# Local attention in a fused decoder: exponentials taken from PSUM, the mask as a factor, output projections at the ends of blocks

## The chip, the core and the metric

The kernel runs on one core of one Trainium2 chip, as one launch. The metric is device time in microseconds, here the median of three runs. A core has engines that run side by side, each working through its own queue in order: TensorE (PE, matrix products; its weight loads are listed apart as PEld), VectorE (DVE), ScalarE (ACT), GpSimd (POOL) and SyncE (SP, which issues DMAs here). PE writes its results to PSUM[...]; DVE and ACT read them from there and write to SBUF.

## What is computed

A decoder with two layers over x of 8 x 512 x 256: layer 0 is self attention, cross attention and a "feed-forward" part that is itself a small transformer of depth 2 with local attention; layer 1 is a quantized attention, a media cross attention and a mixture of experts. All in float32. The change touches the local attention alone, which runs twice:

```
h = shift_token(x); q, k, v = split(h @ wqkv)            # 8 heads of 64
q, k = rotary_xpos(l2norm(q) * qs, l2norm(k) * ksc)
# windows of 128 rows; each query sees its own window and the one before
sim  = einsum(q * 8, k)
mask = (i < j) | (i > j + 128) | (j == -1)
attn = softmax(where(mask, -max, sim))
x = x + (attn @ v) @ wo
```

Since q and k are normalized, the scores are bounded, and the kernel takes no maximum before the exponential.

## The kernel before

The kernel is written with a framework that orders each engine's instructions at build time: it takes those that are ready by its own estimate, by priority, which falls in the order in which the program issues them. Three helpers steer it. `high_priority(AT_ONCE)` lifts instructions over all others. `together` keeps a group of matmuls in one piece behind its first. `in_turn` puts the PE instructions of a thunk behind the newest PE instruction issued so far. Work of a later group that is ready can still be placed ahead of earlier work that is not.

`local_attention(l, y, ahead)` (L1844) is called for l = 0 and 1. It walks 32 blocks, four per batch row (8 rows of the batch; n = 64 heads, two per block). In block `pair` the loop at the end does three things:

- `scores` for two heads of this block (L2017 on): 8 matmuls (16 records, since a float32 matmul is made as two) into two PSUM tiles "sc" of two banks each, keys by queries in tiles of 128 with their 256 (or 128) queries. For each of the two tiles DVE adds the mask (0 or 1e30, L2036, at once) and writes "la_e" to SBUF; ACT makes exp(-x) of that in place (L2040). The queries carry a factor of -8, so that the minus sign is undone. There are six buffers of la_e.
- `weigh` for the two heads of the block before (L2052 on): 8 matmuls with the values into bank "po" (L2047), a copy of it by ACT (L2064), and after every second block 16 matmuls with ones into bank "sum", whose copy by DVE (L2075) goes by DMA to DRAM. There it is reshaped, inverted (L3326) and read back spread over partitions (L3339); POOL multiplies it onto the values (L3340), which gives "la_oT".
- The next batch row's thunks, some of a list of eight groups, one group for each head of the row's blocks (`prepare`, L1958). They are: `turn`, transposes of the input (L1881) with copies by ACT; `project` (L1890), a projection of 128 rows into 512 columns (L1897), evacuated by ACT twice for queries and keys (a square, L1904, and a copy, L1905) and once for values (L1902); `square` and `root` on DVE for the norms; `rotate` (L1924) on DVE, five long operations (L1932 to L1942); `turn_heads` (L1944), transposes of the rotated rows in two halves of four (L1950), each copied by ACT (L1953). The first blocks of a row hold input transposes and query and key projections; the last two hold four times a value projection followed by two halves of transposes.

All of `turn`, `project`, `turn_heads` and `project_out` take their PSUM from two banks "pj", which change hands in turn.

`later` (class Background, L3386) is a list of delayed thunks: each `tick` counts one and runs at most one that is due. A tick stands before each head's group and after each thunk. The four output projections of a batch row (`project_out`, L2087, one for each 128 rows: 8 matmul records, L2090, and an at-once residual add by DVE, L2096) are put on this list 9, 12, 15 and 18 ticks after the last division has begun. In the steady rows each of them lands just before a value projection and its transposes.

The neighbours are the cross attention before layer 0 (its exponential, L1735, and product, L1736, are of the form that the change brings) and the feed-forward `local_ffn` (L2123) after each layer, whose first pieces are run ahead in the last blocks.

Of the kernel before, what the change touches and what calls it, by code (L numbers as in the profile page):

```python
# [33 lines left out]
AF = mybir.ActivationFunctionType  # L34
ALU = mybir.AluOpType
# [4 lines left out]
P = 128  # L40
B, S, C = 8, 512, 256
NST = S // P
NT = B * NST
EPS = 1e-5
BIG = 1e30
# [1232 lines left out]
class FastDecoder(Decoder):  # L1278
# [565 lines left out]
    def local_attention(self, l, y, ahead):  # L1844
# [3 lines left out]
        nc, t = self.nc, self.t  # L1848
        wqkv, wo = self.load_local_attention(l)
        yield  # L1850
        later = Background()
# [9 lines left out]
        scale = self.alloc(first, [P, 2, 64], F32, "la_scale", bufs=1)  # L1861
# [133 lines left out]
        with self.tc.tile_pool(  # L1995
            reuse_waits="tile", name="la", bufs=2, side=sides[1]
        ) as pool, self.tc.tile_pool(reuse_waits="tile", name="lps", bufs=1, space=PSUM) as psum:
            second = pool
            self.pj = lambda: self.alloc(psum, [P, 512], F32, "pj", bufs=2)
            one, two = [P, 512], [P, 2, 512]  # L2000
            if l:
                self.reserve(psum, ("sc", two, 2), ("pj", one, 2), ("po", one, 1), ("sum", one, 1))
            else:
                self.reserve(psum, ("sum", one, 1), ("po", one, 1), ("sc", two, 2), ("pj", one, 2))


            mask = self.alloc(pool, [P, NST, P], F32, "la_mask", bufs=1)
            nc.gpsimd.memset(mask, 0.0)
            for j in range(NST):
                sign = -1 if j % 2 else 1  # L2010
                nc.gpsimd.affine_select(
                    out=mask[:, j, :], in_=mask[:, j, :], pattern=[[sign, P]], compare_op=ALU.is_ge,
                    fill=BIG, base=0, channel_multiplier=-sign,
                )
            mask = mask.rearrange("p j k -> p (j k)")

            def scores(n):  # L2017

                b, c = divmod(n, 4)
                d = held[b]  # L2020
                both = [self.alloc(psum, [P, 2, 512], F32, "sc", bufs=2) for half in range(2)]
                for m in self.together(8):
                    half, jj, r = m // 4, m // 2 % 2, m % 2
                    j = 2 * half + jj
                    to = min((j + 2) * P, S)
                    rows = slice(64 * r, 64 * r + 64)
                    nc.tensor.matmul(  # L2027
                        both[half][:, r, jj * 256 : jj * 256 + to - j * P],
                        d["qkT"][rows, 4 + c, j * P : (j + 1) * P], d["qkT"][rows, c, j * P : to],
                        start=True, stop=True,  # L2030
                    )
                for half, ps in enumerate(both):
                    n_cols = 384 if half else 512
                    ex = self.alloc(pool, [P, 2, 512], F32, "la_e", bufs=6)
                    with self.tc.high_priority(self.AT_ONCE):
                        nc.vector.tensor_tensor(  # L2036
                            ex[:, :, :n_cols], ps[:, :, :n_cols],
                            mask[:, :n_cols].unsqueeze(1).broadcast_to([P, 2, n_cols]), ALU.add,
                        )
                    nc.scalar.activation(ex[:, :, :n_cols], ex[:, :, :n_cols], AF.Exp, scale=-1.0)  # L2040
                    d["e", 2 * c + half] = ex

            def over_keys(out, lhsT, ex, half, jj):

                j = 2 * half + jj
                to = min((j + 2) * P, S)
                nc.tensor.matmul(  # L2047
                    out[:, j * P : to], lhsT(j), ex[:, jj * 256 : jj * 256 + to - j * P],
                    start=(j == 0), stop=(j == 3), skip_group_check=True,
                )  # L2050

            def weigh(n):  # L2052
                b, c = divmod(n, 4)
                d = held[b]
                d["po"] = self.alloc(psum, [P, 512], F32, "po")
                for m in self.together(8):
                    half, jj, r = m // 4, m // 2 % 2, m % 2
                    at = 128 * c + 64 * r
                    over_keys(
                        d["po"][64 * r : 64 * r + 64, :], lambda j: d["v"][:, j, at : at + 64],  # L2060
                        d["e", 2 * c + half][:, r, :], half, jj,
                    )
                o = d["o", c] = self.alloc(pool, [P, S], F32, "la_o", bufs=3)
                nc.scalar.copy(o, d["po"])  # L2064
                if c % 2 == 0:
                    return
                ps = self.alloc(psum, [P, 512], F32, "sum")
                for m in self.together(16):
                    hf, jj, r = m // 8, m // 4 % 2, m % 4
                    over_keys(  # L2070
                        ps[32 * r : 32 * r + 32, :], lambda j: self.ones[:, :32],
                        d["e", 2 * (c - 1 + r // 2) + hf][:, r % 2, :], hf, jj,
                    )
                total = self.alloc(pool, [P, S], F32, "la_total")
                nc.vector.tensor_copy(total, ps)  # L2075

                def divide(rows):
                    for j in range(2):
                        oT = d["oT", c - 1 + j] = self.alloc(pool, [P, S], F32, "la_oT", bufs=6)
                        self.times_rows(pool, oT, d["o", c - 1 + j], rows[2 * j : 2 * j + 2, :], later)  # L2080
                    if c == 3:
                        for i in range(NST):
                            later.add(9 + 3 * i, lambda i=i: project_out(b, i))

                self.inverted(pool, total[0:P:32, :], later, divide)

            def project_out(b, i):  # L2087
                ps = self.pj()
                for c in range(4):
                    nc.tensor.matmul(  # L2090
                        ps[:, :C], held[b]["oT", c][:, i * P : (i + 1) * P], wo[:, c, :],
                        start=(c == 0), stop=(c == 3),
                    )
                yt = y[:, b * NST + i, :]
                with self.tc.high_priority(self.AT_ONCE):
                    nc.vector.tensor_tensor(yt, yt, ps[:, :C], ALU.add)  # L2096

            n = 8 * B
            ahead.step()
            for pair in range(0, n + 2, 2):  # L2100
                if pair < n:
                    if pair % 8 == 0:
                        ready = prepare(pair // 8 + 1) if pair // 8 + 1 < B else [()] * 8
                    scores(pair // 2)
                if pair >= 2:
                    weigh(pair // 2 - 1)
                for i in (pair, pair + 1):
                    with self.in_turn():
                        later.tick(1)
                    if i < n:  # L2110
                        for thunk in ready[i % 8]:
                            with self.in_turn():
                                thunk()
                                later.tick(1)
                    if i == n - 6:
                        early.close()
                    if i > n - 6:
                        with self.in_turn():
                            ahead.step()
            ahead.step(100)  # L2120
            later.drain()

    def local_ffn(self, l, y, ahead):  # L2123

# [1472 lines left out]
```

## Time and profile before

| what | us |
|---|---|
| median of three runs | 3023.35 (3020.69 to 3023.5) |
| the profiled execution | 3023.1 |
| its span, first to last instruction | 3021.3 |
| PE busy | 2819.4 (93%) |
| DVE busy | 2034.0 (67%) |
| ACT busy | 1192.4 (39%) |
| POOL busy | 386.9 (13%) |
| mask additions L2036, 128 | 135.3 |
| exponentials L2040, 128 | 117.6 |

A row of the profile's groups gives line, engine, operation, what it writes and reads, shapes and count, then busy time and mean ns of one, then the engine's idle time before it and what ended that. A row of waits gives who waited for whom, total us, times and longest. A row of the timeline gives start and length in us, engine and line, and in brackets the idle time before it. PE records are pipelined and their ends modelled, so rows of PE overlap a little.

### The profile page before, as it was taken

The numbers are of one execution on the slowest core, as the hardware profiler recorded it, in microseconds if no ns is written. First come the engines' busy times: TensorE is split into PE (matmuls) and PEld (weight loads), VectorE is DVE, ScalarE is ACT, GpSimd is POOL, SyncE is SP. The second block draws the span as 40 slices with busy tenths as digits, with TensorE's granted clock in tenths as the row PEclk, the third lists the DMA queues.
The fourth block names the chain that finished last, engine by engine and source line by source line (L and its number), as shares of the span: only waits on it lengthen the run. The fifth ranks groups of instructions, "written<-read, shape, count | busy, mean of one in ns | idle before, by whom it ended". The sixth has DMA issues, their size and how long they took to land. (4 is left out here: it accounts for less than half of the span.)

```text
span 3021.3 us, 39786 instructions
## 1 busy us (share of the span) xinstructions
PE 2819.4 (93%) x14944; PEld 1507.2 (50%) x14944; DVE 2034.0 (67%) x4546; ACT 1192.4 (39%) x1687; POOL 386.9 (13%) x357
## 2 busy tenths in 40 slices
PE   8999999979999999999999999999796999997998
PEld 5653333334555556555555556554444344444665
DVE  7458999987767784356776788548797766664110
ACT  2237777745444421134444421114363444441111
POOL 1111111100011010000011011111211012121111
PEclk9999999989999999999999999999898999997999
DMA  7011212101000010001000011001332132313331
GB/s 248 1 35 44 78 50 59 46 25 50 16 22 23 22 28 34 1 1 43 16 23 23 16 46 63 21 17 53 113 126 92 43 106 83 108 58 97 106 138 60
DMA packets 130693, 168.71 MB, mean 56 GB/s; under 512 B 51760, under 2 KB 79665, under 8 KB 128442
## 3 DMA queue, kind: packets, MB, share of 16 engines
q1 hardware_dynamic: 126394, 154.48, 16.3%
q0 software_dynamic: 4096, 11.59, 1.1%
q8 instruction: 119, 1.95, 0.3%
q14 instruction: 84, 0.69, 0.1%
HBM read 113.12 MB, written 47.50 MB: 53 GB/s over the span
## 5 line engine op out<-in xcount | busy, mean ns | idle before, releaser
L1897 PE MATMUL pj<-w,la_hT 128*128 128x512 f32 x712 | 330.8, 606 | 11.8 <-DVE x L1790 7.9
L1736 DVE TENSOR_TENSOR x_e<-x_e,x_share 128x1024 f32<-128x1024 f32 x256 | 316.1, 1278 | 13.5 <-ACT x_e L1735 13.4
L1735 ACT ACTIVATE x_e<-sc 128x1024 f32<-128x1024 f32 x256 | 249.2, 1023 | 78.6 <-PE sc L1724 78.6
L1897 PEld LDWEIGHTS pj<-w,la_hT 128*128 128x128 f32 x712 | 131.3, 191 | 157.2 <-issue 110.0
L2036 DVE TENSOR_TENSOR la_e<-sc,la_mask 128x1024 f32<-128x1024 f32 (+1 forms) x128 | 135.3, 1082 | 104.1 <-PE sc L2027 103.9
L2965 ACT ACTIVATE ma_e<-sc,ma_bias 128x1024 f32<-128x1024 f32 x128 | 135.9, 1111 | 145.7 <-PE sc L2959 132.2
L3340 POOL TENSOR_TENSOR la_oT<-la_o,x_wide 128x512 f32<-128x512 f32 x64 | 98.0, 1545 | 736.0 <-DMA x_wide<-invs 569.3
L2253 ACT ACTIVATE lf_gate<-pj,lf_b 128x512 f32<-128x512 f32 (+1 forms) x82 | 56.3, 687 | 334.5 <-PE pj L2232 327.3
L2040 ACT ACTIVATE la_e<-la_e 128x1024 f32<-128x1024 f32 (+1 forms) x128 | 117.6, 946 | 152.0 <-DVE la_e L2036 151.0
L2232 PE MATMUL pj<-lf_hnT,w 128*128 128x512 f32 (+1 forms) x368 | 171.4, 593 | 1.8 <-DVE lf_hid L2258 1.8
L1752 PE MATMUL po<-x_e,x_v 128*32 128x512 f32 x1024 | 137.3, 608 | 24.4 <-DVE x_e L1736 19.7
L2232 PE MATMUL sc<-lf_hnT,w 128*128 128x512 f32 x336 | 157.7, 592 | 0.0
L1724 PE MATMUL sc<-x_q,x_k 32*128 32x512 f32 x1024 | 151.1, 639 | 1.7 <-DVE sa_ok L1448 1.4
L2304 PE MATMUL po<-w,lf_hid 128*128 128x256 f32 x640 | 149.0, 379 | 0.0
L2258 DVE SCALAR_TENSOR_TENSOR lf_hid<-sc,lf_b,lf_gate 128x512 f32<-128x512 f32 x70 | 52.4, 748 | 136.6 <-PE sc L2232 136.6
L2047 PE MATMUL po<-la_e,la_v 128*64 128x256 f32 (+1 forms) x1024 | 124.8, 368 | 7.1 <-ACT la_o L2064 6.4
L2027 PE MATMUL sc<-la_qkT 64*128 64x256 f32 (+1 forms) x1024 | 128.0, 373 | 2.5 <-DVE la_e L2036 1.9
L2304 PEld LDWEIGHTS po<-w,lf_hid 128*128 128x128 f32 x640 | 117.8, 190 | 21.2 <-issue 7.4
L2959 PE MATMUL sc<-ma_qT,ma_kT 64*128 64x512 f32 x512 | 127.4, 615 | 0.4 <-ACT ma_e L2965 0.4
L2982 PE MATMUL po<-ma_e,ma_v 128*64 128x512 f32 x512 | 125.7, 612 | 0.0
L2090 PE MATMUL pj<-w,la_oT 128*128 128x256 f32 x512 | 121.9, 385 | 2.0 <-DVE lf_t L1480 0.7
L1913 DVE TENSOR_REDUCE la_ss<-la_sq 128x16 f32<-128x1024 f32 x64 | 77.6, 1214 | 66.2 <-ACT la_sq L1904 66.2
(509 smaller groups left out, 5162.1 us busy)
## 6 DMA issues: line engine op xcount, KB each, us to landing
x_wide<-invs SPq DMA_DIRECT2D x184, 128.0 KB
w<-in_f_w_dram SPq DMA_DIRECT2D x16, 1024.0 KB
kv<-kv_o SPq DMA_DIRECT2D x56, 256.0 KB
slots<-x_empty SPq DMA_DIRECT2D x8, 1028.0 KB
x_mask<-in_x_maskT_dram SPq DMA_DIRECT2D x8, 1024.0 KB
ma_kT<-kv SPq DMA_DIRECT2D x8, 1024.0 KB
ma_v<-kv SPq DMA_DIRECT2D x8, 1024.0 KB
ex_rows<-slots SPq DMA_DIRECT2D x7, 1028.0 KB
```

The lines of the kernel that those rows point to most:

```text
L1724: nc.tensor.matmul(pair[r // 2][:, r % 2, :], d["k"][rows, g, kt * P : (kt + 1) * P], d["q"][rows, e, g, :], start=True, stop=True,)
L1735: nc.scalar.activation(ex, d["e"][rest][p], AF.Exp)
L1736: nc.vector.tensor_tensor(ex, ex, d["share"][:, kt, :].unsqueeze(1).broadcast_to([P, 2, 512]), ALU.mult)
L1752: nc.tensor.matmul(d["po"][32 * r : 32 * r + 32, :], d["v"][:, kt, 8 * g + 2 * r + e, :], ex[r // 2][:, r % 2, :], start=(kt == 0), stop=( ...
L1897: nc.tensor.matmul(ps, d["hT"][:, k, i * P : (i + 1) * P], wqkv[:, k, j * S : (j + 1) * S], start=(k == 0), stop=(k == 1),)
L2027: nc.tensor.matmul(both[half][:, r, jj * 256 : jj * 256 + to - j * P], d["qkT"][rows, 4 + c, j * P : (j + 1) * P], d["qkT"][rows, c, j * P ...
L2036: nc.vector.tensor_tensor(ex[:, :, :n_cols], ps[:, :, :n_cols], mask[:, :n_cols].unsqueeze(1).broadcast_to([P, 2, n_cols]), ALU.add,)
L2232: nc.tensor.matmul(ps[:m, :], w1[:, k, at : at + m], held[b]["hnT"][:, k, :], start=(k == 0), stop=(k == 1))
L2304: nc.tensor.matmul(ps[:, :C], held[b]["hid"][:, f, i * P : (i + 1) * P], w2[:, f, :], start=(f == 0), stop=False,)
L2959: nc.tensor.matmul(both[m // 2][:, r, :], d["k"][rows, c, kt * P : (kt + 1) * P], d["q"][rows, c, :], start=True, stop=True,)
L2965: nc.scalar.activation(ex, ps, AF.Exp, bias=bias[:, b * NST + kt : b * NST + kt + 1], scale=0.125)
L2982: nc.tensor.matmul(d["po"][64 * r : 64 * r + 64, :], d["v"][:, kt, 128 * c + 64 * r : 128 * c + 64 * r + 64], exs[m // 2][:, r, :], start= ...
```

## The change

The mask holds ones and zeros in place of zeros and 1e30. ACT takes the exponential from the PSUM tile and writes la_e to SBUF; DVE multiplies la_e by the mask in place, without the raised priority. The output projections of a batch row are no longer on the list of delayed thunks: two ticks after the last division has begun, all four are entered in a list `due`, and a block takes none, one, one or two from it (by its place in the row) after its two heads' thunks. The steps that run the feed-forward's first pieces ahead move into a loop of their own behind that. What is left in `due` is issued at the very end.

```diff
-            nc.gpsimd.memset(mask, 0.0)
+            nc.gpsimd.memset(mask, 1.0)
...
-                    fill=BIG, base=0, channel_multiplier=-sign,
+                    fill=0.0, base=0, channel_multiplier=-sign,
...
                     ex = self.alloc(pool, [P, 2, 512], F32, "la_e", bufs=6)
-                    with self.tc.high_priority(self.AT_ONCE):
-                        nc.vector.tensor_tensor(
-                            ex[:, :, :n_cols], ps[:, :, :n_cols],
-                            mask[:, :n_cols].unsqueeze(1).broadcast_to([P, 2, n_cols]), ALU.add,
-                        )
-                    nc.scalar.activation(ex[:, :, :n_cols], ex[:, :, :n_cols], AF.Exp, scale=-1.0)
+                    nc.scalar.activation(ex[:, :, :n_cols], ps[:, :, :n_cols], AF.Exp, scale=-1.0)
+                    nc.vector.tensor_tensor(
+                        ex[:, :, :n_cols], ex[:, :, :n_cols],
+                        mask[:, :n_cols].unsqueeze(1).broadcast_to([P, 2, n_cols]), ALU.mult,
+                    )
...
                     if c == 3:
-                        for i in range(NST):
-                            later.add(9 + 3 * i, lambda i=i: project_out(b, i))
+                        later.add(2, lambda: due.extend((b, i) for i in range(NST)))
...
             ahead.step()
+            due = []
             for pair in range(0, n + 2, 2):
...
                                 thunk()
                                 later.tick(1)
+                for tile in due[: (0, 1, 1, 2)[pair // 2 % 4]]:
+                    with self.in_turn():
+                        project_out(*tile)
+                    due.remove(tile)
+                for i in (pair, pair + 1):
                     if i == n - 6:
                         early.close()
...
             later.drain()
+            for tile in due:
+                project_out(*tile)
```

## The prediction

> **What bounds the kernel now.** I read the page's busy rows first: TensorE (PE) is busy 93% of the span, VectorE (DVE) 67%, ScalarE (ACT) 39%. Then the page's groups, to find the two local-attention stages: layer 0's scores start at 680.6 us and its last output projection at about 1130, layer 1's run from some 1380 to 1816. Then the time by stretches of 52 us, about one batch row, in layer 0:
>
> ```profile
> core 0: us, PE busy (x) PEld busy (x) DVE busy (x) ACT busy (x) POOL busy (x), PEclk, DMA share, GB/s
> 690.00:742.00 52.00, 46.47 (x312) 26.49 (x312) 43.15 (x64) 26.73 (x43) 5.47 (x5) 1.00 0.07 22
> 846.00:898.00 52.00, 49.43 (x291) 29.05 (x292) 39.77 (x62) 24.77 (x42) 6.86 (x5) 1.00 0.08 22
> 898.00:950.00 52.00, 48.70 (x298) 28.24 (x295) 39.50 (x61) 23.56 (x41) 6.27 (x4) 1.00 0.08 22
> ```
>
> Here too PE sets the pace: it is idle 2.6 to 5.5 us of 52, ACT works half the time, and the change moves no work onto or off PE. So the change can win only PE's idle time, and it loses only what it adds to it. The waits of PE alone, layer 0 (690 to 1110 us) and then layer 1 (1390 to 1810), say whose that is:
>
> ```profile
> PE pj L1950 <- DVE x L2096: 16.5, 16, 1.6
> PE po L2047 <- ACT la_o L2064: 4.1, 2, 3.8
> PE pj L1950 <- ACT la_qkT L1953: 2.8, 1, 2.8
> ...
> PE pj L1950 <- DVE x L2096: 14.5, 16, 1.7
> PE po L2047 <- ACT la_o L2064: 2.3, 2, 2.1
> PE pj L1950 <- ACT la_qkT L1953: 2.2, 1, 2.2
> ```
>
> The transposes of the heads (L1950) wait 31.0 us in 32 places for the residual add of an output projection (L2096). The timeline shows one of them whole:
>
> ```profile
> 872.36 1.99 PE L2090 MATMUL pj<-w,la_oT 128*128 128x256 f32 x8
> 874.19 1.88 PE L1897 MATMUL pj<-w,la_hT 128*128 128x512 f32 x4
> 875.25 1.22 DVE L1941 TENSOR_TENSOR la_qk<-la_qk,la_cos 128x1024 f32<-128x1024 f32 x1
> 876.38 0.41 DVE L2096 TENSOR_TENSOR x<-x,pj 128x256 f32<-128x256 f32 x1
> 876.85 0.66 PE L1950 MATMUL pj<-ident,la_qk 128*128 128x128 f32 x4 [0.78 <-DVE x L2096]
> ```
>
> There are two pj banks. The output projection takes one, the projection after it the other, and the transposes need the first again. Its add is urgent by priority, yet DVE works in order: it begins 2.0 us after the projection of the output has ended, behind a rotation already queued, and the 1.9 us of one projection on PE do not cover that. The pattern repeats three times in each batch row. It is not the rotation itself that the transposes wait for: in the steady rows the rotated heads (L1942) are ready 2.97 to 6.4 us before the transposes start, by the starts and ends in the timeline.
>
> **Output projections at block ends.** Per batch row there are four: now each comes in front of a projection and its transposes. After the change one ends block 1, one block 2, two block 3. I sort the 32 waits by the transposes they delay. Before the first pair of a row: ten waits, 10.3 us in all (0.52 to 1.61 each). Before the second: ten of 1.04, 10.4. Before the third: ten of about 0.70 and two of 1.64 and 1.65, 10.3. The sum is the 31.0.
> - The projection that ends block 1 is followed by the next block's scores, values and sums, 16, 16 and 32 matmul records of 1.79, 1.74 and 1.72 us: 5.2 us of PE on other banks, against an add that ends at most 2.9 + 0.4 us late. The first wait goes: 10.3.
> - Nothing is put before the second projection and transposes any more: 10.4 go.
> - The one that ends block 2 should also be followed by scores. But today PE's order pulls the next block's scores and values forward, between the two halves of the transposes (scores stand at 877.44, between halves at 876.85 and 879.15). If they stay pulled forward, this output projection again stands straight before a projection and transposes. I count the third 10.3 as staying. The other end would be nothing.
> - Each wait also costs the refill of PE: the projection above starts at 874.19 and its four matmuls follow at 0.429, so the next could start at 875.90; it started at 876.85, 0.95 late where the row says 0.78. Twenty waits gone x 0.16 is 3.2.
> - The two that end block 3 come just before the transposes of the next row's input, which need both banks. By then DVE is nearly idle and the add starts 0.04 us after its projection (at 895.74 after 895.70) and takes 0.41, while four transposes take 0.45. Nothing to 0.5 for each of 14 rows; I take 0.
>
> Sum of this part: -10.3 - 10.4 - 3.2 = -23.9 us.
>
> **Exponential from PSUM, mask by multiplication.** 128 mask additions (1218 ns at 1024 wide, 947 at 768) become multiplications, 128 exponentials (1058 and 835 ns) now read PSUM. The nearest rows are the kernel's own cross attention, which already does this: its exponential from PSUM takes 1023 ns, its multiplication in SBUF 1278. So ACT gets 64 x 0.035 = 2 us shorter at most, DVE 64 x 0.06 = 4 longer and about as much at 768. Neither is the bound and I count 0 for both. What covers DVE's part is the 2.97 us by which rotated heads are early; without that cover the 8 us would be PE's.
>
> One rule speaks against the multiplication. The Trainium skill, page "SBUF — State Buffer", section "Who interferes with whom", says that a VectorE instruction with two SBUF inputs contends with a GpSimd instruction that reads SBUF, through a shared port. The mask addition has one input in PSUM; the multiplication has two in SBUF. The trace agrees: sorted by overlap with a GpSimd instruction, the 1024-wide additions take 1222 ns with and 1217 without, cross attention's multiplications 1645 with and 1209 without. Of the 64 wide additions 13 overlap; if both widths do so as often, 26 x 0.44 = 11 us in two stages, some 0.8 per batch row. By the additions' row it would be 0. I take 11 on DVE and 0 on the path, again under the 2.97.
>
> Order matters more than length. Now the chain is scores, DVE, ACT, values; DVE's queue holds the addition up, ACT waits behind it (75.0 us in layer 0 and 67.2 in layer 1, up to 4.5), and copies queued behind the exponential on ACT wait too. That cost PE the 2.8 and 2.2 us above: the copy of the turned heads stood behind an exponential that waited for its mask. After the change ACT waits for PE alone, and both go: -5.0. I leave the 3.2 us of projections that waited for the same copy as they are.
>
> The new chain adds a wait on DVE: the multiplication waits for the exponential, and rotations, square sums and residual adds are queued behind it. It lost its priority. Its own reader has time: values are weighed a block later, 11 us or more after the scores (scores from 891.94 to 902.7, their values at 913.82). The new cost on ACT: two exponentials (1.06 + 0.84) now come straight after the scores, hence between the copies of turned heads. A copy can be 1.9 us late, of which a 1.72 us projection covers most. Bounds are 0 and 0.6 for each of two places per batch row; 0.3 x 28 = +8.4.
>
> Sum: 3023.1 (the profiled execution, 1.8 over its span, 0.25 under the median) - 23.9 - 5.0 + 8.4 = 3002.6. PE's later stages start earlier by this, and PE is busy in them too. I say 3002.
>
> **The rivals.**
> *All waits go* (0.20): the scheduler leaves scores and values behind the block-2 output projection, ACT costs nothing. 31.0 + 32 x 0.16 + 5.0 + the 3.2 = 44: 2979. For it: scores wait for fewer things. Against: they stand early today.
> *The wait changes its name* (0.17): an output projection between transposes and projection also gave ACT time. Without it, projection, transposes, projection run at the pace of ACT's copies: the second half waits for a copy of 0.59 under 0.45 us of transposes, the next projection for the first half's copy. About 0.3 + 0.2 at four places in 14 rows is 28 instead of 8.4: 3022. Against it: today every such gap holds scores or values.
> *Slower* (0.17): DVE stands still at the multiplication. In each of the three busy blocks it waits 1.06 us for the first exponential and about 0.9 for copies ahead of that on ACT: 3 x 1.96 = 5.9 per row. From 2.97 on, by which the rotated heads are early, it goes straight to PE: 2.9 + 0.1 of contention x 14 = 42. Then 3002.6 - 8.4 + 42 = 3036. For it: DVE is busy 22 to 25 of 26 us in half of each row. Against it: the scheduler can put ready rotations ahead.
> The likeliest case has 0.46.
>
> **How the numbers follow.** About 0.2% (6 us) is what a measurement of this kernel can tell from no change. The likeliest case alone spans 2994 (no ACT cost) to 3013 (the second wait stays too). Adding the full gain below and the changed wait above gives 2979 to 3028, which leaves most of the slower case out. Faster 0.67 (likeliest and full gain, plus a little), same 0.17, slower 0.16.
>
> **What would show it.** Right: L2096's wait before the transposes falls from 32 places to about 12, ACT no longer waits for DVE before its exponentials, and PE is busy about 1.7 us more of each steady 52. Wrong, the first rival: no such wait left. Second: transposes and projections waiting for ACT copies by 20 us or more. Third: transposes waiting for rotations, and DVE idle before multiplications with ACT named. The prediction falls if PE's order, made by the scheduler, comes out so that pj banks are asked for in another sequence.

## The result, and the profile after

The changed kernel takes 3035.49 us (median of 6, 3033.03 to 3038.97) against 3023.43 beside it: ratio 1.0037, 95% interval 1.0026 to 1.0047. It is slower by 12 us where I forecast 21 us less. Its profiled execution took 3035.97 with a span of 3034.2; the granted clock's mean over the span is 0.967 where it was 0.977.

First the three stretches that the prediction shows, layer 0:

```profile
core 0: us, PE busy (x) PEld busy (x) DVE busy (x) ACT busy (x) POOL busy (x), PEclk, DMA share, GB/s
690.00:742.00 52.00, 46.44 (x288) 26.16 (x285) 40.01 (x59) 24.21 (x41) 3.00 (x3) 0.93 0.07 17
846.00:898.00 52.00, 48.69 (x291) 28.34 (x290) 40.96 (x61) 23.49 (x39) 5.58 (x5) 0.97 0.08 22
898.00:950.00 52.00, 48.18 (x290) 29.15 (x288) 39.79 (x61) 23.86 (x39) 6.16 (x4) 0.98 0.08 22
```

PE is not 1.7 us busier per stretch, as it had to be. It is busy as long as before or less, and part of that is slow work: the granted clock was 1.00 in all three and is now 0.93, 0.97 and 0.98. The waits of PE, layer 0 and then layer 1:

```profile
PE pj L1950 <- DVE x L2094: 17.9, 5, 4.2
PE pj L1950 <- DVE la_qk L1942: 8.6, 2, 5.4
PE po L2046 <- ACT la_o L2063: 5.5, 1, 5.5
...
PE pj L1950 <- DVE x L2094: 17.2, 5, 4.2
PE pj L1950 <- DVE la_qk L1942: 5.7, 3, 3.2
```

The waits for the residual add (now L2094) still cost 35.1 us, where they cost 31.0. But these are 10 places and not 32: two of three waits per row went, as forecast, the third stayed, as forecast, and grew from about 0.70 us to 3.2 to 4.2. The copies of turned heads (L1953) that cost 2.8 and 2.2 are gone. One of the ten in the timeline, PE first and then DVE:

```profile
938.99 1.89 PE L2088 MATMUL pj<-w,la_oT 128*128 128x256 f32 x8
940.72 1.88 PE L1897 MATMUL pj<-w,la_hT 128*128 128x512 f32 x4
946.38 0.66 PE L1950 MATMUL pj<-ident,la_qk 128*128 128x128 f32 x4 [3.78 <-DVE x L2094]
```

```profile
941.07 1.18 DVE L1941 TENSOR_TENSOR la_qk<-la_qk,la_cos 128x1024 f32<-128x1024 f32 x1
942.17 1.22 DVE L2036 TENSOR_TENSOR la_e<-la_e,la_mask 128x1024 f32<-128x1024 f32 x1
943.30 1.22 DVE L1942 TENSOR_TENSOR la_qk<-la_qk,la_r 128x1024 f32<-128x1024 f32 x1
944.44 0.95 DVE L2036 TENSOR_TENSOR la_e<-la_e,la_mask 128x768 f32<-128x768 f32 x1
945.31 0.68 DVE L1938 TENSOR_TENSOR la_r<-la_qk,la_sin 128x512 f32<-128x512 f32 x1
945.91 0.42 DVE L2094 TENSOR_TENSOR x<-x,pj 128x256 f32<-128x256 f32 x1
```

The output projection ended at 940.88. Its add starts 5.0 us later, behind these five operations and a reciprocal of 0.25 us, with no gap in DVE. In the kernel before, the third wait of the same batch row looked like this:

```profile
943.00 1.89 PE L2090 MATMUL pj<-w,la_oT 128*128 128x256 f32 x8
946.83 0.42 DVE L2096 TENSOR_TENSOR x<-x,pj 128x256 f32<-128x256 f32 x1
947.30 0.66 PE L1950 MATMUL pj<-ident,la_qk 128*128 128x128 f32 x4 [0.70 <-DVE x L2096]
```

There the output projection ended at 944.89 and its add came 1.9 us later. Over the steady rows the add was 1.9 us late in this place before, and is 4.4 to 5.5 late now. Two of the five operations are products of one block's scores. What follows such a wait stands in the stretches around it:

```profile
942.60:946.40 3.80, 0.02 (x2) 0.02 (x1) 3.80 (x6) 0.59 (x1) 0.01 (x1) 1.00 0.42 121
947.50:951.00 3.50, 3.46 (x12) 2.08 (x11) 3.47 (x2) 1.77 (x3) 2.77 (x2) 0.51 0.00 0
951.00:954.50 3.50, 3.50 (x19) 1.66 (x19) 1.48 (x2) 1.07 (x2) 0.10 (x1) 1.00 0.00 0
```

PE stands for 3.80 us, resumes, and a microsecond later has 3.5 us at clock 0.51. From the first to the last score of each layer (814 us for both layers together, 796 before) the clock was halved for 72 us, against 7.5 before. The page's groups for the mask:

```profile
L2036 DVE TENSOR_TENSOR la_e<-la_e,la_mask 128x1024 f32<-128x1024 f32 (+1 forms) x128 | 138.0, 1092 | 90.5 <-ACT la_e L2035 90.5
L2035 ACT ACTIVATE la_e<-sc 128x1024 f32<-128x1024 f32 (+1 forms) x128 | 112.3, 917 | 80.3 <-PE sc L2027 80.1
```

The exponential now waits for PE alone, as forecast. The 128 products take 138.0 us where the additions took 135.3: the operation itself has become hardly dearer.

### The profile page after: what moved, and what is told of

Read it like the earlier page. It is cut to its first block, busy times and chain, and to the rows that moved or that the text cites. A ratio compares the mean times of both kernels' runs of the same rounds, so it can differ in the third digit from the quotient of the medians.

```text
span 3034.2 us, 39837 instructions
## 1 busy us (share of the span) xinstructions
PE 2827.5 (93%) x14929; PEld 1520.6 (50%) x14944; DVE 2057.8 (68%) x4546; ACT 1189.4 (39%) x1687; POOL 384.1 (13%) x357
## 5 line engine op out<-in xcount | busy, mean ns | idle before, releaser
L1897 PE MATMUL pj<-w,la_hT 128*128 128x512 f32 x712 | 337.6, 617 | 8.2 <-DVE x L1790 7.9
L1736 DVE TENSOR_TENSOR x_e<-x_e,x_share 128x1024 f32<-128x1024 f32 x256 | 315.9, 1277 | 12.9 <-ACT x_e L1735 12.8
L2036 DVE TENSOR_TENSOR la_e<-la_e,la_mask 128x1024 f32<-128x1024 f32 (+1 forms) x128 | 138.0, 1092 | 90.5 <-ACT la_e L2035 90.5
L2035 ACT ACTIVATE la_e<-sc 128x1024 f32<-128x1024 f32 (+1 forms) x128 | 112.3, 917 | 80.3 <-PE sc L2027 80.1
L2027 PE MATMUL sc<-la_qkT 64*128 64x256 f32 (+1 forms) x1024 | 135.0, 394 | 0.5 <-ACT la_e L2035 0.3
L1950 PE MATMUL pj<-ident,la_qk 128*128 128x128 f32 x468 | 83.1, 306 | 49.4 <-DVE x L2094 35.1
```

The lines of the kernel that those rows point to most:

```text
L1736: nc.vector.tensor_tensor(ex, ex, d["share"][:, kt, :].unsqueeze(1).broadcast_to([P, 2, 512]), ALU.mult)
L1897: nc.tensor.matmul(ps, d["hT"][:, k, i * P : (i + 1) * P], wqkv[:, k, j * S : (j + 1) * S], start=(k == 0), stop=(k == 1),)
L2027: nc.tensor.matmul(both[half][:, r, jj * 256 : jj * 256 + to - j * P], d["qkT"][rows, 4 + c, j * P : (j + 1) * P], d["qkT"][rows, c, j * P ...
L2036: nc.vector.tensor_tensor(ex[:, :, :n_cols], ex[:, :, :n_cols], mask[:, :n_cols].unsqueeze(1).broadcast_to([P, 2, n_cols]), ALU.mult,)
```

## The experiments

The question is which part made PE's third wait grow: the list of output projections, the product, its lost priority, or the order of PE's queue that came out of them. One view carries most of what follows. Each PE record's time to the next start is set against the mean of the same pair of records, over all traces, where there is neither a wait nor a half clock; what lies above is put to the wait in front of the next record, or to the half clock. This is worked out from the traces, over the score stretches of both layers. The columns are those of the profiled execution, which for some kernels lies off the median: it took 3001.3 us for "after, no product", 3018.4 for "after, addition unhurried" and 3005.6 for "after, product at once". What is left is called "work". The same 4560 PE records stand in these stretches in every kernel (84 more, 36 us, in "filled wait"), and yet this column runs from 728 to 751: so much the method does not resolve, and a difference of less than some 20 us between two kernels proves nothing here.

```
kernel                          median us   waits  half clock  work
before                            3023.4     50.3      3.8    741.9
after                             3035.5     53.5     31.6    728.1
mask alone                        3047.1     62.0     17.9    734.9
projections alone                 3018.6     43.0      2.0    750.8
after, 0,2,0,2                    3035.7     45.6     29.1    735.1
after, product at once            3011.2     38.0      6.5    739.8
after, filled wait                3028.2     31.4      5.7    766.8
after, addition unhurried         3011.0     39.9      4.2    746.6
mask alone, product at once       3050.6     69.3     19.5    737.6
at once, 0,2,0,2                  3026.8     41.8     18.6    739.3
after, sums by ACT                3057.3     68.2     28.8    727.6
addition, sums by ACT             3042.8     58.8     24.9    732.0
after, no product                 2988.2     24.1     12.9    730.5
addition, 0,2,0,2                 3016.6     44.4      1.9    747.3
after, scores early               2994.1     26.7      0.4    742.1
after, scores early, at once      2996.5     27.9      0.7    742.1
before, scores early              3034.2     54.0      9.1    741.9
```

**The mask alone**, on the kernel before:

```diff
-                    with self.tc.high_priority(self.AT_ONCE):
-                        nc.vector.tensor_tensor(
-                            ex[:, :, :n_cols], ps[:, :, :n_cols],
-                            mask[:, :n_cols].unsqueeze(1).broadcast_to([P, 2, n_cols]), ALU.add,
-                        )
-                    nc.scalar.activation(ex[:, :, :n_cols], ex[:, :, :n_cols], AF.Exp, scale=-1.0)
+                    nc.scalar.activation(ex[:, :, :n_cols], ps[:, :, :n_cols], AF.Exp, scale=-1.0)
+                    nc.vector.tensor_tensor(
+                        ex[:, :, :n_cols], ex[:, :, :n_cols],
+                        mask[:, :n_cols].unsqueeze(1).broadcast_to([P, 2, n_cols]), ALU.mult,
+                    )
```

> The mask part alone; output projections stay on the delayed list, so PE's order is the old one with three output projections per row in front of a projection and transposes. Theory A (backlog: VectorE runs late in the second half of each row, and PE's waits for residual adds, once taken away, gather in the one that is left, 3.2 to 4.2 us, which is long enough to halve the granted clock behind it): the waits stay spread, about 30 places of about 1 us, the clock stays at about 0.977, the time is 3015 to 3025. Theory B (the product itself, without priority and in front of the residual adds, makes the adds late): the 30 waits grow by 1 to 2 us each, 3050 or more, and the clock falls.

Measured: 3047.09 us, ratio 1.0069 (1.0055 to 1.0083). Waits of PE for the add (L2095 here), both layers:

```profile
PE pj L1950 <- DVE x L2095: 21.4, 14, 2.4
...
PE pj L1950 <- DVE x L2095: 23.4, 12, 2.5
```

The mask's part alone costs 22 us against the 3024.92 beside it. The waits have kept their places and are longer; the longest now halve the clock (17.9 us in the table).

**The projections alone**, with addition and exponential as before:

```diff
-                        for i in range(NST):
-                            later.add(9 + 3 * i, lambda i=i: project_out(b, i))
+                        later.add(2, lambda: due.extend((b, i) for i in range(NST)))
...
+                for tile in due[: (0, 1, 1, 2)[pair // 2 % 4]]:
+                    with self.in_turn():
+                        project_out(*tile)
```

> The output projections alone at block ends, mask added as before and at once. Theory A: one long wait per row for the residual add of the projection that ends block 2, 2 to 4 us, unless values stand before the transposes in PE's order; granted clock below the old 0.977, 3025 to 3040. Theory B: that wait is 0.7 to 1 us, the clock stays, about 3003 as predicted for the order alone.

Measured: 3018.59 us, 0.9975 (0.9965 to 0.9985): faster by 6, between the two expectations. The adds' waits went altogether, and the copies of turned heads came in their place: L1950 waits 11.6 and 11.0 us for L1953, 7 times a layer. So the loss comes with the mask's part: with the new list it costs some 17 us, on the old one 22.

**No output projection in block 2**:

```diff
-                for tile in due[: (0, 1, 1, 2)[pair // 2 % 4]]:
+                for tile in due[: (0, 2, 0, 2)[pair // 2 % 4]]:
```

> The changed kernel with the output projections as none, two, none, two in a row's four blocks: none is left in front of the row's third projection and transposes. Theory A: the wait of 3.2 to 4.2 us for the add goes; what is late next is the rotated head, up to 1.9 us; no stretch of half clock per row, so 12 rows win some 2 us of waiting and 1.7 to 3.4 of clock: 2985 to 3005, clock back at about 0.977. Rival: the backlog shows at the rotated heads in full, as another wait of 3 us and more, the clock stays at 0.967 and the time within 6 us of the changed kernel's 3035.

Measured: 3035.69 us, 1.0036 (1.0023 to 1.0048), no better than after. The wait is in the same place under another name, layer 0 and layer 1:

```profile
PE pj L1950 <- DVE la_qk L1942: 22.9, 7, 5.5
...
PE pj L1950 <- DVE la_qk L1942: 19.5, 7, 2.9
```

With no add to wait for, the third transposes wait for their own rotated head, 2.9 us each in the steady rows. So the wait needs no add: DVE as a whole is behind there. The comparison is not a pure one, since PE's order moved too: four score records now stand between the third projection and its transposes.

**The product at once**: the product inside the raised priority that the addition had.

```diff
+                    with self.tc.high_priority(self.AT_ONCE):
                         nc.vector.tensor_tensor(
                             ex[:, :, :n_cols], ex[:, :, :n_cols],
```

> The changed kernel with the product at raised priority, as the mask addition had it. Theory B: the two products leave the place in front of the residual add, its lateness falls from 4.4-5.5 to about 2.3 us, the wait to about 1, the clock returns: about 3000. Theory A: VectorE has as much to do before the add, only in another order, and the wait or one for a rotated head stays over 3 us: 3030 to 3040.

Measured: 3011.19 us, 0.9955 (0.9941 to 0.9969). It lies between the two expectations and beats both kernels, but not evenly: the wait for rotated heads (L1942) is 20.7 us in layer 0 and 9.8 in layer 1, seven times in each. The two layers run the same code. What differs is PE's order, which is settled when the kernel is built. From the traces, a steady row by runs of records (turn: input transposes, sc: scores, p: projection, t: head transposes, po: values, PO: output projection):

```
late (after):
 turn8 sc16 p16 po16 p16 PO8 sc16 po16 sum32 p4 t4 sc16 t4 p4 t4 po16 t4
 PO8 p4 t4 sc8 t4  p4 t4 po6 sc4 po10 t4 PO4 sc4 PO12 sum32
early (product at once, layer 1; projections alone):
 turn4 sc16 turn4 p2 sc16 p30 PO8 po16 sum32 p4 t4 sc16 t4 p4 t4 po16 t4
 PO8 p4 sc4 po16 t8 ...
```

In the early order two blocks' scores are issued before all but two records of the row's projections, when DVE is least loaded, and one pair of products is left in DVE's full stretch ahead of the third add. The last pair of scores and a block's values then stand between the third projection and its transposes. In the late order the second block's scores come after the projections; two pairs of products fall into DVE's full stretch ahead of that add, and nothing stands between that projection and its transposes. Layer 0 of this kernel lies between the two. The kernel before has the late order as well, with an output projection in front of each of the four projections.

**The wait filled**: three matmuls whose result nothing reads, behind the projection that precedes the long wait.

```diff
-                [one((p, 2, 2), (r, 3)), one((t, 2))],
+                [one((p, 2, 2), (fill,), (r, 3)), one((t, 2))],
...
+            for k in range(3):
+                nc.tensor.matmul(ps, self.ident, wqkv[:, 0, 0:S], start=True, stop=True)
```

> The changed kernel plus useless work: three extra matmuls (six records, 2.6 us) of the identity with a weight into the idle sum bank, in each row right after the third value projection, so that TensorE works through most of the wait of 3.2 to 4.2 us for the residual add. Nothing reads them. Theory C (the clock): waits of 2.9 us and more halve the granted clock behind them, 72 us at half speed in the two stages against 7.5 before, worth 32 us, which is what the forecast lacks. Then the extra work makes the kernel faster: half-clock time in the stages under 20 us, clock about 0.977, 3005 to 3013. Rival (VectorE's backlog sets the length of a row and the clock is only a companion): 3030 to 3040 as before, whatever the clock.

Measured: 3028.24 us, 1.0014 (1.0007 to 1.0020), between the two expectations. The stretch of 846 us shows the clock restored:

```profile
846.00:898.00 52.00, 50.08 (x299) 28.85 (x299) 40.65 (x60) 23.92 (x40) 5.58 (x5) 1.00 0.07 22
```

Yet of 26 us of half-clock loss only 7 come back as time. The third transposes start no sooner than in after, 40.9 to 42.0 us behind the row's first transposes of the input, and the fourth now wait 1.0 to 1.2 us for their rotated heads in nearly every steady row, where in after they did not (waits for rotated heads: 8.8 us in layer 0, 10.0 in layer 1). With PE at full clock, DVE sets the pace of this half row; most of what the halved clock takes, PE would have stood waiting. PE's order is that of after but for one block's last scores, which moved from between the two halves of the third transposes to behind them.

**The addition without hurry**: the new list, with the old addition and no raised priority for it.

```diff
-                    with self.tc.high_priority(self.AT_ONCE):
-                        nc.vector.tensor_tensor(
+                    nc.vector.tensor_tensor(
```

> Output projections at block ends, the mask as an addition from PSUM ahead of the exponential as in the kernel before, but without the raised priority. If priority is what the new form lost (theory B): long waits per row as in the changed kernel, clock near 0.967, 3030 to 3040. If it is the order exponential first, product second that matters: like the version with the urgent addition, 3015 to 3022.

Measured: 3011.01 us, 0.9953 (0.9941 to 0.9966), less than either expectation, in the early order; waits of L1950 for L1953 12.1 and 11.5 us. The addition without priority is no worse than with it: lost priority is not the cause.

**The product at once on the old list**: the mask alone, with the priority.

```diff
+                    with self.tc.high_priority(self.AT_ONCE):
                         nc.vector.tensor_tensor(
```

> The mask part alone as in the first experiment, with the product at raised priority; output projections on the old delayed list. Theory B: the waits of up to 2.4 us and the half-clock stretches of that experiment (38 us in the stages) go, 3018 to 3027, as the kernel before or a little less since copies on ScalarE no longer stand behind the mask. Otherwise (products in front of residual adds at any priority): 3040 to 3050.

Measured: 3050.55 us, 1.0087 (1.0072 to 1.0101); waits for the add 25.9 and 27.8 us. PE's order is that of the kernel before. Here the priority helps nothing, so on the new list it helped through the order that came with it.

**At once, none in block 2**: both edits together.

```diff
+                    with self.tc.high_priority(self.AT_ONCE):
                         nc.vector.tensor_tensor(
...
-                for tile in due[: (0, 1, 1, 2)[pair // 2 % 4]]:
+                for tile in due[: (0, 2, 0, 2)[pair // 2 % 4]]:
```

> The changed kernel with the product at raised priority and output projections as none, two, none, two. With the raised priority alone, the third transposes of a row wait for their rotated heads, 1.4 us in layer 1 and 2.6 in layer 0, and not for the residual add. Theory A (VectorE's backlog): taking the projection away brings TensorE to that wait 1.7 us sooner, the wait grows by that to 3 us and more in layer 0, half clock returns there: 3010 to 3025. Rival (the add was still part of the wait): 2995 to 3005.

Measured: 3026.80 us, 1.0010 (1.0002 to 1.0019), just above the first range. By accident this is the cleanest comparison: one kernel, layer 0 with its second block's values ahead of its scores, layer 1 in the early order.

```profile
PE pj L1950 <- DVE la_qk L1942: 23.2, 7, 5.0
...
PE pj L1950 <- DVE la_qk L1942: 8.6, 7, 2.1
```

Half clock: 38.9 us in layer 0, 3.4 in layer 1; the score stretches take 409.3 and 390.7 us, where before took 401.1 and 395.4. So the order alone moves a layer by 18.6 us, or 12.9 less the 5.7 by which the layers differ before; the change moved them by 9.4 and 7.9.

**Sums copied by ACT**, in after, to take their copies off DVE:

```diff
-                nc.vector.tensor_copy(total, ps)
+                nc.scalar.copy(total, ps)
```

> The changed kernel with the copies of the row sums on ScalarE in place of VectorE (0.69 us each, one of them ahead of the residual add that the third transposes wait for). TensorE's order stays that of the changed kernel: a block's scores come behind the row's projections, so that two pairs of products lie in VectorE's full stretch. Theory A (VectorE's backlog in the second half of a row sets the third wait, the clock doubles the harm): the wait of 3.2 to 4.2 us falls by about 0.7 to 2.5-3.5, half clock in most rows still, 3025 to 3032. Rival (the backlog is not the cause): unchanged, 3033 to 3038.

Measured: 3057.26 us, 1.0111 (1.0095 to 1.0126), 22 us worse than after. The waits for the add are 28.2 and 27.7 us, 6 in each layer. In the trace PE's order is the late one still, but the add is queued an operation or two further back on DVE, after the next L1939. A miss: less work on DVE did not help while the operation PE wants stands further back. It isn't settled that this accounts for all 22; the two score stretches are only 11 us longer than in after.

**The addition with sums by ACT**: the unhurried addition with the same edit.

```diff
-                nc.vector.tensor_copy(total, ps)
+                nc.scalar.copy(total, ps)
```

> As the one before, with the mask as an addition ahead of the exponential, without raised priority. With the sums on ScalarE TensorE's order comes out the same as with the product, scores late. Theory A' (what made the versions with the addition faster is TensorE's order, with a block's scores pulled between the input's transposes, so that one pair of mask operations instead of two lies in VectorE's full stretch): no such order here, so within 8 us of the product's version. Rival (the form itself: product behind the exponential is worse for VectorE than the addition): 3008 to 3018, clock 0.977.

Measured: 3042.82 us, 1.0062 (1.0049 to 1.0076); L1950 waits 23.1 and 21.0 us, 7 times a layer, for the copies L1953. This kernel came out in the late order, and 32 us slower than the unhurried addition in the early one. That late order hurts the addition too is likely but not shown by this: the sums' copies moved as well, and in after that move alone cost 22 us without a change of order. Beside the run above, product against addition in the late order costs 14 us; 3042.82 is outside both expectations.

**No product**: after without its multiplication, so that every query attends to all keys of its two windows.

```diff
-                    nc.vector.tensor_tensor(
-                        ex[:, :, :n_cols], ex[:, :, :n_cols],
-                        mask[:, :n_cols].unsqueeze(1).broadcast_to([P, 2, n_cols]), ALU.mult,
-                    )
```

> The changed kernel without the multiplication by the mask: the mask is left out, every query attends to all keys of its two windows. TensorE's order is the changed kernel's. Theory A: VectorE loses two pairs of 2.17 us ahead of the third add, the wait of 3.2 to 4.2 goes to nearly nothing, the clock returns to 0.977, 2988 to 3002. Rival (order of queues, not the amount of VectorE's work): the wait stays over 2 us, half clock stays, 3020 to 3035.

Measured: 2988.18 us (2982.98 to 3001.26), 0.9876 (0.9861 to 0.9891), 47 us under after; the trace is of the slowest execution, 35 under.

```profile
846.00:898.00 52.00, 50.32 (x310) 30.21 (x309) 30.87 (x53) 24.80 (x42) 5.18 (x5) 1.00 0.07 22
```

DVE is busy 31 us of 52 and not 41, and PE 50.3 and not 48.7. Waits for the add are down to 10.9 and 9.9 us, six a layer of about 1.7. DVE's load is what the long wait is made of, though DVE is idle a fifth of the row in after. The run takes away more than the products: the rotations, which in after lose 27 us where they overlap with GpSimd's work, lose about 1 here.

**The addition, none in block 2**: the unhurried addition with 0, 2, 0, 2.

```diff
-                for tile in due[: (0, 1, 1, 2)[pair // 2 % 4]]:
+                for tile in due[: (0, 2, 0, 2)[pair // 2 % 4]]:
```

> The mask as an addition without raised priority, output projections as none, two, none, two: scores early in TensorE's order. With one, one, two the version took 3011. Theory A: the third transposes already wait for nothing long there, so taking the projection away changes little: 3005 to 3015, clock 0.975 or more. Rival: as with the product and late scores, the rotated heads take the wait over, 3018 to 3030.

Measured: 3016.59 us, 0.9973 (0.9962 to 0.9983), just above the first range, against 3011.0 for 0, 1, 1, 2: with the addition in the early order the list is worth 6 us. With the product it was 4.5 us in the one layer that had the early order in both runs (390.7 against 386.2).

**Scores early**: after, with the early order written into the code. The second block's scores are issued behind the row's first thunk, the third's behind its third.

```diff
+            early_scores = set()
...
-                    scores(pair // 2)
+                    if pair // 2 not in early_scores:
+                        scores(pair // 2)
...
                                 thunk()
                                 later.tick(1)
+                            if i % 8 == 0 and thunk in (ready[0][0], ready[0][2]):
+                                ahead_by = 1 if thunk is ready[0][0] else 2
+                                early_scores.add(i // 2 + ahead_by)
+                                scores(i // 2 + ahead_by)
```

> The changed kernel, product without raised priority, with the scores of a row's second and third block issued right behind the first transposes of the input and behind the first projection: TensorE's order becomes that of the three fastest versions (scores early), in both layers. Theory D (the order decides: with scores late, two pairs of products lie in VectorE's full stretch ahead of the third residual add; with scores early only one): the third wait falls to about 1.5 us, no half clock, 2993 to 3005. Rival (the raised priority made the fast version fast): the wait stays over 2.5 us, 3020 to 3035.

Measured: 2994.11 us (2993.52 to 2994.39), 0.9901 (0.9886 to 0.9916), the best of all that compute everything: 41 us under after, 31 under before. Its stretches, and the place of the old long wait, PE and then DVE:

```profile
846.00:898.00 52.00, 50.53 (x303) 29.58 (x300) 40.34 (x62) 24.55 (x41) 5.72 (x6) 1.00 0.08 22
898.00:950.00 52.00, 50.56 (x300) 29.35 (x300) 40.97 (x62) 24.02 (x41) 4.15 (x4) 1.00 0.07 21
```

```profile
1494.85 1.89 PE L2088 MATMUL pj<-w,la_oT 128*128 128x256 f32 x8
1496.58 1.88 PE L1897 MATMUL pj<-w,la_hT 128*128 128x512 f32 x4
1498.39 0.70 PE L2027 MATMUL sc<-la_qkT 64*128 64x256 f32 x4
1499.02 1.73 PE L2046 MATMUL po<-la_e,la_v 128*64 128x256 f32 x16
1502.05 0.66 PE L1950 MATMUL pj<-ident,la_qk 128*128 128x128 f32 x4 [1.29 <-DVE la_qk L1942]
```

```profile
1499.69 0.42 DVE L2094 TENSOR_TENSOR x<-x,pj 128x256 f32<-128x256 f32 x1
```

DVE is as full as in after (40.3 and 41.0 us of 52), and the add is still 2.95 us late (1499.69 after 1496.74). But 2.4 us of scores and values cover it, the wait that is left is short, and the clock stays at 1.00. The same run speaks against contention with GpSimd as the cause: the rotations lose 27 us to it as in after, 10 of the 64 wide products are slowed where it was one, and the kernel is 41 us faster.

**Scores early and at once**: the same with the raised priority.

```diff
+                    with self.tc.high_priority(self.AT_ONCE):
                         nc.vector.tensor_tensor(
```

> The same with the product at raised priority. Theory D: within 6 us of the version without the priority, 2993 to 3005. Rival (priority matters): faster than it by 15 us or more.

Measured: 2996.52 us, 0.9913 (0.9899 to 0.9926). With the order fixed, the priority gains nothing.

**Scores early in the kernel before**, with its addition and its old list: the same edit.

```diff
+                            if i % 8 == 0 and thunk in (ready[0][0], ready[0][2]):
...
+                                scores(i // 2 + ahead_by)
```

> The kernel before the change, with nothing but the same earlier issue of two blocks' scores. Three output projections per row still stand in front of a projection and transposes. Theory D: VectorE is rid of one pair of mask additions in its full stretch, the waits for residual adds fall from 31 us to 15-25, 3005 to 3017. Rival (the place of the output projections is what counts): 3020 to 3028.

Measured: 3034.24 us, 1.0034 (1.0022 to 1.0046): the waits as forecast, the time a miss. Layer 0:

```profile
PE pj L1950 <- DVE x L2096: 10.1, 6, 1.8
PE sc L2027 <- DVE la_e L2036: 8.4, 2, 8.1
PE pj L1897 <- ACT la_qkT L1953: 6.4, 6, 1.6
```

The add's waits fall from 31.0 to 20.3 (10.1, and 10.2 in layer 1). Against that stand 12.8 us in both layers of waits for copies of turned heads, which queue on ACT behind an exponential that itself waits for the mask, and one wait of 8.1 us with a half clock after it. PE's order is the early one in the first half of the row alone: in the second half the output projections still stand straight in front of a projection and its transposes, with no scores or values to cover the adds. So early scores by themselves are no gain; with the new list the addition had both halves of the early order and took 3011 to 3019 us. What more this kernel loses stays open; the rotations' loss beside GpSimd is 29 us in it, where before lost 14.

## Why the prediction was wrong, point by point

- **First and second wait go: right.** Of 32 waits for the add 10 are left, in the third place.
- **The third wait stays at about 0.70 (10.3 us): the step that failed.** That PE keeps the scores pulled forward, with the output projection straight in front of projection and transposes, was right. Wrong was to take the wait's size from before. I counted, in ten steady rows of each trace, from a row's first transposes of the input. PE's third output projection ends at 36.2 us where it ended at 40.5, so 4.4 us sooner: two waits with their refill are gone, and one output projection has moved to the row's end. DVE, whose operations stand without a gap from the row's second sum of squares to its last rotation, starts the add at 40.9 where it was 42.5, only 1.6 us sooner. The wait takes up the difference, 3.2 to 4.2 us in place of 0.70, and the sum is 35.1 us in place of 31.0. The early order shows that this need not be: there scores and values cover it.
- **The 2.97 us by which rotated heads are early: lost by the same step.** They were early because PE came late. In the wait shown above the third rotated head is done at 944.52, and PE had been ready since 942.60: without any add the transposes would still have waited 1.9 us, and in "no output projection in block 2" they wait 2.9.
- **The clock: no term in the sum.** Of the 32 short waits before, 0.5 to 1.65 us long, one was followed by a half clock. Now the long waits halve it for 72 us (31.6 us of PE's time in the table, against 3.8). It hides partly behind DVE: with it restored, and PE's order kept but for one block's scores, the time falls by 7 us.
- **Refill, -3.2:** not tested by itself; too small beside these.
- **ACT no longer behind the mask, -5.0: right.** The 2.8 and 2.2 us are gone. Of the 8.4 us for late copies nothing shows: no row names a wait of PE for them.
- **The product, 11 us of contention: mis-sized.** The 128 take 138.0 us against 135.3. The rule of the Trainium skill ("SBUF — State Buffer", section "Who interferes with whom") holds in part of the overlaps: of the 64 wide products six overlap with GpSimd's work and one is slowed. The rotations, with two SBUF inputs as well, lost 27.3 us over their undisturbed durations, against 14.3 before: more of GpSimd's work falls on them now. That sits inside DVE's full stretch, but the kernel with scores early carries it too.
- **That DVE's wait for the exponential would do it:** the rival gave 3036 and the time is 3035, but it was right in the number only, which is luck. DVE's idle time before products is 45.4 us in layer 0, against 51.3 before the additions, and in the steady rows none of it lies in the gapless stretch. DVE isn't held up by waiting there; a pair of products stands ahead of what PE wants.

The chance left for slower, 0.16, priced one mechanism. What I named last, that PE's order made at build might come out otherwise, is the larger risk: the changed kernel with nothing but its scores issued earlier took 2994 us in place of 3035.

What stays open is what the product costs where PE's order does not move: on the old list it took 22 us, and the runs show longer waits, halved clock and products that come later on DVE than the additions did, but not what each of these is worth.

## What to carry to other kernels

Where two engines share a row, ask for each wait removed how far the later engine is behind at the next place. If it has no gap, the wait can move and grow, as here, and a long one halved PE's clock where several short ones mostly had not. When a change takes an operation to another engine, compare PE's issue order of both builds before crediting either operation. Write the order down in the code if the time hangs on it: scores issued where DVE is free turned the same change from +0.4% into -1.0%.

## What the runs showed of the hardware that was not expected

How long PE may be idle before its clock is halved. Over the idle times of PE in the local stages of 14 traces (all but the three with scores early), the clock fell to about half within 7 us of the end of 1 in 86 idle times of 1.0 to 1.5 us, 12 in 57 of 1.5 to 2.0, 42 in 61 of 2.0 to 3.0, and 45 in 46 of 3.0 or more. A half stretch lasted 3.4 or 6.8 us. The Trainium skill ("TensorE: Matmul & The Clock Gate", section "HAM oscillation — how this bites in real kernels") warns of gaps above some 3.4 us; here two thirds of that was mostly enough. The counts say how often the two came together, not that the idle time alone did it. And a VectorE operation with one input in PSUM was no dearer than with both in SBUF: 1217 ns for the wide addition, 1209 to 1221 for the wide rotations, both without overlap with GpSimd.
